# A state space layer on one core: ScalarE's work planned in a list of its own, products moved to other places, B's rows sent ahead of C's

## The chip, the cores and the metric

One core of a Trainium2 chip. The metric is the device time of the program in microseconds (us), the median of several executions. Ratios are computed as the mean time of one kernel's fast runs over the mean of the kernel before's fast runs of the same rounds, so they are not quite the ratio of the medians that stand beside them.

## The reference, cut to what matters

The program is two residual layers on an image of 4 x 384 x 64 x 64, float32: a state space layer, then attention over 7 x 7 windows. Only the first is touched.

```python
xn = layer_norm(group_norm(x))                  # 4 x 4096 positions x 384
xb, z = split(xn @ in_proj_w.T)                 # 768 channels each
xc = silu(conv4(xb) + conv_b)
dt, Bm, Cm = split(xc @ x_proj_w.T)             # 24, 16, 16
dt = softplus(dt @ dt_w.T + dt_b)
A = -exp(A_log)                                 # 768 x 16
def step(h, dt_t, B_t, C_t, x_t):               # over 4096 positions
    h = exp(dt_t[:, :, None] * A) * h + (dt_t * x_t)[:, :, None] * B_t[:, None, :]
    return h, sum_n(h * C_t)                    # 16 states n
y = (scan(step) + xc * D) * silu(z)
out = x + y @ out_proj_w.T
# ... then the attention layer, unchanged
```

## The kernel before

The layer runs in 64 *steps* (4 batches x 16 chunks of T = 256 positions). A step has 6 blocks of 128 channels (`d`) x 4 groups of 4 states (`g`), so 24 pairs (d, g), numbered `m`; each is scanned in two *halves* of two states. So a step has 48 halves, and one VectorE scan of 128 x 513 belongs to each.

For one half ScalarE makes two exponentials, VectorE scans; for one `m` there is one product dt x B (128 x 1024), 15 of the 24 on VectorE and 9 on GpSimd; GpSimd multiplies the states by C and TensorE sums them over the states into `y`. What VectorE reads lies in two PSUM tiles of two banks each. Half 0 of every `m` uses the first tile's exponentials, half 1 the second's; the copy of dt x for block `d` lies in tile `d % 2`:

```python
pairs  = [ps_a.tile([P, 4 * T], F32, name=f"pair_{k}") for k in range(2)]
dtx_ps = [t[:, 0:T] for t in pairs]             # dt x, copied there by ScalarE
da_ps  = [t[:, T : 3 * T + 1] for t in pairs]   # two exponentials

def driven(I, m, h, eng):                       # dt x B
    d, g = divmod(m, NS // NG)
    dtx = dtx_ps[d % 2] if eng is nc.vector else h["dtx"][d]
    eng.tensor_tensor(states(dbs[I, m]), dtx..., h["B"][g]..., ALU.mult)

def decay(I, m, half, h):                       # the two exponentials of a half
    for k in range(2):
        act(da_ps[half][:, k*(T+1) : k*(T+1) + T], h["dt"]..., AF.Exp, scale=...)

def scans(I, m, half, hs):
    nc.vector.tensor_tensor_scan(hs[:, half, :], da_ps[half], dbs[I, m][:, half, :], ...)
```

Everything else of a step (norms, projections, convolution, softplus, gating, output) is cut into small pieces, and a plan says after which half each piece is emitted. An engine executes its instructions in the order in which they are emitted here, so the plan *is* the schedule:

```python
plan = [[[] for _ in range(SLOTS)] for _ in range(STEPS + 3)]     # SLOTS = 48
driven_at = ((-4, 0), (-1, 1), (1, 1), (2, 1), ...)   # (half, on VectorE?) of each dt x B
turn(I, p, h, slot_of(I), (p + 1) * (SLOTS // 3) + 4, (3, 2, 4)[p])   # y leaves PSUM, p of 3
# ...
for half in range(2):
    decay(*nxt, steps[nxt[0]])       # exponentials of the next half
    if half == 0:
        with_c(*behind[-1])          # GpSimd: states x C
        for _ in range(ready):
            summed(*behind.pop(0))   # TensorE: sums of y
    scans(I, m, half, hs)            # VectorE
    run(I, 2 * m + half, 2 * m + half + 1)   # what is planned in this half
```

## Time and profile before

| kernel before | |
|---|---|
| time, median of 3 (lowest, highest) | 8,390.1 us (8,385.0, 8,392.5) |
| a usual step, from scan to scan 48 later | 92.4 us |
| of which VectorE idles (mean of steps 10 to 59) | 6.2 us |
| first and last scan of the layer | 117.9 and 6,044.3 us |

The step's length and the idle time by half come from counting scans off in the trace, 48 at a time, and adding VectorE's gaps before each instruction by the half in which it stands. A line of a timeline holds start, us, engine, line, operation, how many in a row. The busy line of the page (engine, us, share of the span, number of instructions) is needed again for the result:

```profile
PE 7235.9 (86%) x45882; PEld 5481.4 (65%) x45882; DVE 7052.0 (84%) x10231; ACT 5936.5 (71%) x15294; POOL 6966.1 (83%) x5719
```

ScalarE's largest waits between 1,000 and 5,000 us (who waited, for whom: us in total, times, longest):

```profile
ACT pair L96 <- DVE hs L594: 316.9, 536, 3.2
ACT pair L96 <- DVE db L575: 302.8, 172, 3.7
```

An exponential waits either for the scan that reads its tile, or for a product that reads the dt x part of the same tile. ScalarE is not the bound, so this costs nothing by itself. It says how tightly the two engines are laced together: whoever moves a product moves exponentials.

TensorE's timeline shortly before scan 20 of step 30, which starts at 2,940.66 (start, us, engine, line, operation, how many in a row).

```profile
2936.97 1.04 PE L623 MATMUL y<-ident,hs 128*128 128x128 f32 x8
2937.84 1.46 PE L389 MATMUL mm_ps<-xn,w_in 128*128 128x256 f32 x6
2939.14 1.46 PE L668 MATMUL mm_ps<-yg,w_out 128*128 128x256 f32 x6
2940.43 1.04 PE L623 MATMUL y<-ident,hs 128*128 128x128 f32 x8
```

The last eight matmuls finish a third of `y`. They are emitted in half 18, behind six matmuls of half 16 and six of half 17, and here they start 0.23 us *before* scan 20 (1.6 us before it in the median of steps 10 to 59). ScalarE copies this `y` out of PSUM in half 20, and right behind it on ScalarE stands the dt x copy that lies in the tile that scan 21 reads.

### The profile page before, as it was taken

To read this page: it belongs to the slowest core of one execution; us is meant where nothing else is said; L and a number is where in the kernel's file an instruction comes from. 1 tells how busy PE (TensorE), PEld (TensorE's weight loads), DVE (VectorE), ACT (ScalarE), POOL (GpSimd) and SP (SyncE) were. 2 spreads that over 40 slices of the span, in tenths; PEclk is the share of its full clock that TensorE was granted. 3 is DMA by queue.
4 is the path that set the end of the run, shared out by engine and by line. 5 is a ranking of instruction groups with operands and counts; after the bars stand their busy time and mean duration, and the time that the engine had idled before them with its cause. 6 is when DMAs were issued, how large, how long until landed. Compare 5 with 4: busy or idle time off the path is not lost.

```text
span 8390.6 us, 137885 instructions
## 1 busy us (share of the span) xinstructions
PE 7235.9 (86%) x45882; PEld 5481.4 (65%) x45882; DVE 7052.0 (84%) x10231; ACT 5936.5 (71%) x15294; POOL 6966.1 (83%) x5719
## 2 busy tenths in 40 slices
PE   6888888888888888888888888888699999999999
PEld 5766677667666766676667766767555555555555
DVE  5999999999999999999999999999756666666666
ACT  5788787878887788788878888888545455455455
POOL 4898898988998898898989898989767677777677
PEclk9998998888988898988899889998799999999999
DMA  3112211121112112211211111112132232232222
GB/s 108 63 59 65 75 59 54 62 73 59 62 65 73 52 57 64 74 57 64 68 62 52 56 64 62 53 58 69 63 92 87 76 96 86 78 91 85 83 87 65
DMA packets 327496, 582.99 MB, mean 69 GB/s; under 512 B 62940, under 2 KB 211180, under 8 KB 326660
## 3 DMA queue, kind: packets, MB, share of 16 engines
q1 hardware_dynamic: 326788, 574.17, 21.9%
q8 instruction: 369, 6.05, 0.3%
q14 instruction: 339, 2.78, 0.1%
HBM read 471.49 MB, written 84.73 MB: 66 GB/s over the span
## 4 chain that ended last, share of the span: by engine, by line
PE 29%; ACT 21%; DVE 19%; POOL 18%; issue 12%; DMA 0%; SPq 0%; POOLq 0%; DVEq 0%; ACTq 0%
POOL hs L607 11%; DVE hs L594 10%; ACT pair L96 10%; POOL db L575 5%; DVE db L575 4%; PE pt_ps L981 4%; PE lg_ps L950 3%; PE mm_ps L854 3%; PE mm_ps L1034 3%; PE mm_ps L887 3%; PE mm_ps L917 3%; PE pv_ps L1007 3%; PE pt_ps L995 2%; ACT spe L96 2%; ACT xc L96 1%
## 5 line engine op out<-in xcount | busy, mean ns | idle before, releaser
L594 DVE TENSOR_TENSOR_SCAN hs<-pair,state,db 128x513 f32<-128x513 f32 x2880 | 3570.7, 1272 | 279.5 <-ACT pair L96 136.5
L96 ACT ACTIVATE pair<-dt,nega 128x256 f32<-128x256 f32 x6144 | 2922.3, 477 | 1051.3 <-DVE hs L594 476.7
L607 POOL TENSOR_TENSOR hs<-hs,C 128x1024 f32<-128x1024 f32 x1536 | 3491.4, 2273 | 124.2 <-POOL state L604 0.6
L623 PE MATMUL y<-ident,hs 128*128 128x128 f32 x12288 | 1839.9, 302 | 755.5 <-POOL hs L607 725.5
L623 PEld LDWEIGHTS y<-ident,hs 128*128 128x128 f32 x12288 | 1580.4, 156 | 1107.3 <-POOL hs L607 948.0
L971 POOL TENSOR_SCALAR sg<-sg,rsum 128x308 f32<-128x308 f32 x1536 | 1623.0, 1075 | 637.4 <-DVE rsum L969 632.7
L575 POOL TENSOR_TENSOR db<-dtx,B 128x1024 f32<-128x1024 f32 x576 | 1368.1, 2375 | 0.4 <-ACT db L568 0.4
L389 PE MATMUL mm_ps<-xn,w_in 128*128 128x256 f32 x4608 | 1187.0, 404 | 93.3 <-ACT xb L96 62.3
L575 DVE TENSOR_TENSOR db<-pair,B 128x1024 f32<-128x1024 f32 x960 | 1153.2, 1207 | 68.5 <-ACT pair L96 68.5
L389 PEld LDWEIGHTS mm_ps<-xn,w_in 128*128 128x128 f32 x4608 | 908.1, 205 | 230.4 <-ACT xb L96 76.0
L96 ACT ACTIVATE sg<-sg,mx 128x308 f32<-128x308 f32 x1536 | 828.7, 540 | 251.4 <-DVE mx L956 224.1
L956 DVE CUSTOM_DVE_ANT_0 sg<-lg_ps,bias 128x308 f32<-128x308 f32 x1536 | 643.2, 475 | 382.5 <-PE lg_ps L950 382.5
L396 PE MATMUL mm_ps<-xb,dcv 128*128 128x256 f32 x3072 | 744.4, 389 | 111.2 <-DVE dt L527 107.0
L396 PEld LDWEIGHTS mm_ps<-xb,dcv 128*128 128x128 f32 x3072 | 578.3, 193 | 213.3 <-DVE dt L527 129.2
L604 POOL COPY state<-hs 128x4 f32<-128x4 f32 x1536 | 292.6, 190 | 477.8 <-DVE hs L594 464.6
L999 ACT COPY tb<-pt_ps 88x512 f32<-88x512 f32 x384 | 222.2, 579 | 624.7 <-PE pt_ps L995 624.7
L668 PE MATMUL mm_ps<-yg,w_out 128*128 128x256 f32 x2304 | 529.5, 380 | 0.0
L986 DVE COPY ta<-pt_ps 110x512 f32<-110x512 f32 x768 | 492.7, 683 | 23.3 <-PE pt_ps L981 23.3
L668 PEld LDWEIGHTS mm_ps<-yg,w_out 128*128 128x128 f32 x2304 | 428.6, 190 | 53.2
L981 PE MATMUL pt_ps<-ident,sg 128*110 128x128 f32 x3072 | 417.6, 279 | 0.9 <-POOL sg L971 0.8
L546 POOL TENSOR_TENSOR dtx<-dt,xc 128x256 f32<-128x256 f32 x384 | 281.6, 733 | 122.6 <-DVE dt L527 122.6
L981 PEld LDWEIGHTS pt_ps<-ident,sg 128*110 128x110 f32 x3072 | 322.7, 133 | 78.1 <-issue 49.0
(145 smaller groups left out, 9301.3 us busy)
## 6 DMA issues: line engine op xcount, KB each, us to landing
B<-bcrows SPq DMA_DIRECT2D x256, 512.0 KB
C<-bcrows SPq DMA_DIRECT2D x256, 512.0 KB
vw<-vd SPq DMA_DIRECT2D x1792, 33.0 KB
xr<-x SPq DMA_DIRECT2D x28, 1056.0 KB
vd<-v SPq DMA_DIRECT2D x280, 96.0 KB
xi<-in_x_dram SPq DMA_DIRECT2D x64, 384.0 KB
xo<-in_x_dram SPq DMA_DIRECT2D x64, 384.0 KB
x<-xo SPq DMA_DIRECT2D x64, 384.0 KB
```

The source lines that it names most:

```text
L96: ins = nc.scalar.activation(o, i, func, **kw)
L389: nc.tensor.matmul(pb[:, k, :], w_in[:, j, m * P : (m + 1) * P], xn[:, j, :], start=(j == 0), stop=(j == NJ - 1),)
L396: nc.tensor.matmul(pb[:, k, :], dcv[:, d, c, :], xb[:, d, c : c + T], start=(c == 0), stop=(c == KC - 1),)
L575: eng.tensor_tensor(states(db), dtx.unsqueeze(1).unsqueeze(1).broadcast_to([P, 2, 2, T]), h["B"][g].rearrange("p (a k) t -> p a k t", k=2) ...
L594: nc.vector.tensor_tensor_scan(hs[:, half, :], da_ps[half], dbs[I, m][:, half, :], state[d][g][:, 2 * half : 2 * half + 1] if I % NCHUNK e ...
L607: nc.gpsimd.tensor_tensor(by_state, by_state, h["C"][g].rearrange("p (a k) t -> p a k t", k=2), ALU.mult)
L623: nc.tensor.matmul(y[:, d % 2, half, :], hs[:, k // 2, at : at + P], ident, is_transpose=True, start=(first and half == 0 and d % 2 == 0), ...
L668: nc.tensor.matmul(h["po", first][:, m - first, :], w_out[:, d, m * P : (m + 1) * P], h["yg"][d // 2][:, d % 2, :], start=(d == 0), stop=( ...
L956: nc.vector.tensor_tensor_reduce(sg[:, hh, :], lg[:, :NK], bias[:, 4 * m + hh, :], -1.0, BIG, ALU.add, ALU.min, mx[:, hh : hh + 1],)
L971: nc.gpsimd.tensor_scalar(sg[:, hh, :], sg[:, hh, :], rs[:, hh : hh + 1], None, ALU.mult)
L981: nc.tensor.transpose(pt[: KN[c], col : col + P], sg[:, 2 * pair + hh, KOFF[c] : KOFF[c] + KN[c]], ident,)
L986: nc.vector.tensor_copy(t[: KN[0], :, :].rearrange("p a q -> p (a q)"), pt[: KN[0], :])
```

## The change

The intent, in its author's words: ScalarE's other work between exponentials and spread, dt x B laid where ScalarE has much to do, B transferred ahead of C. No instruction is added or removed. Each half of the plan gets two lists, one for ScalarE's work and one for the rest; multi-part ScalarE pieces are split so that single instructions can go between two exponentials; the places of dt x B are new.

```diff
+            ACT = 1
...
-                at(22, by_group)
+                for j in range(NJ):
+                    at(22 + j, lambda j=j: by_group(j), ACT)
...
-                at(35, root)
+                at(34, logged, ACT)
+                at(35, root, ACT)
...                             (biases, softplus parts: split in the same way)
-                    for tag in "BBBCBCCC":
+                    for tag in "BBBBCCCC":
...
-            plan = [[[] for _ in range(SLOTS)] for _ in range(STEPS + 3)]
+            plan = [[([], []) for _ in range(SLOTS)] for _ in range(STEPS + 3)]
...
-                def at(s, what):
-                    plan[I + s // SLOTS][s % SLOTS].append(what)
+                def at(s, what, kind=0):
+                    plan[I + s // SLOTS][s % SLOTS][kind].append(what)
...
             driven_at = (
-                (-4, 0), (-1, 1), (1, 1), (2, 1), (4, 0), (7, 1), (8, 0), (10, 1),
-                (12, 0), (15, 1), (17, 1), (18, 1), (20, 0), (22, 1), (24, 0), (26, 1),
-                (27, 1), (27, 1), (30, 0), (33, 1), (36, 0), (39, 1), (40, 0), (43, 1),
+                (-4, 0), (-2, 1), (-2, 1), (-1, 1), (3, 0), (5, 1), (7, 0), (7, 1),
+                (11, 0), (14, 1), (18, 1), (20, 1), (20, 0), (22, 1), (23, 0), (26, 1),
+                (27, 1), (28, 1), (30, 0), (32, 1), (36, 0), (38, 1), (39, 1), (40, 0),
             )
...
                 for half in range(2):
+                    acts, others = plan[I][2 * m + half]
                     if 2 * n + half + 1 < len(halves):
                         nxt = halves[2 * n + half + 1]
-                        decay(*nxt, steps[nxt[0]])
+                        acts.insert(0, lambda nxt=nxt: decay(*nxt, 0, steps[nxt[0]]))
+                        acts.insert(2, lambda nxt=nxt: decay(*nxt, 1, steps[nxt[0]]))
+                    for what in acts:
+                        what()
                     if half == 0:
...                             (states x C, sums of y: as before)
                     scans(I, m, half, hs)
-                    run(I, 2 * m + half, 2 * m + half + 1)
+                    for what in others:
+                        what()
```

One line does something other than it says. `at` files ordinary work under index 0 and ScalarE's under index 1; the loop unpacks index 0 as `acts`. So the list that is emitted between the exponentials, ahead of the scan, is the *ordinary* one.

More of the change, by code (lines that the diff above doesn't have):

```diff
@@ L346, in load, with by_group @@
                     )
-                def by_group():
-                    h["xn"] = w2.tile([P, NJ, T], F32, tag="xn", name=f"xn_{b}_{i}", bufs=1)
-                    for j in range(NJ):
-                        act(
-                            h["xn"][:, j, :], h["x"][:, j, :], AF.Identity,
-                            scale=gms[b][:, j, 1:2], bias=gbs[b][:, j, :],
-                        )
+                def by_group(j):
+                    if j == 0:
+                        h["xn"] = w2.tile([P, NJ, T], F32, tag="xn", name=f"xn_{b}_{i}", bufs=1)
+                    act(
+                        h["xn"][:, j, :], h["x"][:, j, :], AF.Identity,
+                        scale=gms[b][:, j, 1:2], bias=gbs[b][:, j, :],
+                    )
                 def mean(of, key):
@@ L371, in square, with logged @@
                     act(h["sq"], h["xn"], AF.Square)
+                def logged():
+                    act(h["var"][:, 0, :], h["var"][:, 0, :], AF.Ln, bias=eps)
                 def root():
-                    act(h["var"][:, 0, :], h["var"][:, 0, :], AF.Ln, bias=eps)
                     act(h["var"][:, 0, :], h["var"][:, 0, :], AF.Exp, scale=-0.5)
                 at(12, load)
-                at(22, by_group)
+                for j in range(NJ):
+                    at(22 + j, lambda j=j: by_group(j), ACT)
                 at(25, lambda: mean("xn", "mu"))
                 at(27, lambda: with_row("mu", ALU.subtract))
-                at(30, square)
+                at(30, square, ACT)
                 at(32, lambda: mean("sq", "var"))
-                at(35, root)
+                at(34, logged, ACT)
+                at(35, root, ACT)
                 at(36, lambda: with_row("var", ALU.mult))
@@ L399, in conv, with with_bias @@
                     )
-            def with_bias(dst, pb, bias):
-                for k in range(2):
-                    act(dst[:, k, :], pb[:, k, :], AF.Identity, bias=bias[:, k : k + 1])
+            def with_bias(k, dst, pb, bias):
+                act(dst[:, k, :], pb[:, k, :], AF.Identity, bias=bias[:, k : k + 1])
             def prepared(I, h, at):
@@ L436, in prepared, with x_out, conv_out, z_out @@
                     pair(("x", p), x, lambda pb, k, d=d: in_proj(pb, k, d + k, h["xn"]))
-                    at(x[2], lambda p=p, d=d: with_bias(
-                        xb[:, d : d + 2, KC - 1 :], h["pb"][("x", p)], binp[:, d : d + 2]
-                    ))
-                    def conv_out(p=p, d=d):
-                        c = w2.tile([P, 2, T], F32, tag="xc", name=f"xc_{b}_{i}_{d}", bufs=6)
-                        with_bias(c, h["pb"][("c", p)], cvb[:, d : d + 2])
-                        h["xc"].append(c)
-                    pair(("c", p), c, lambda pb, k, d=d: conv(pb, k, d + k))
-                    at(c[2], conv_out)
-                    def z_out(p=p, d=d):
-                        z = w2.tile([P, 2, T], F32, tag="sz", name=f"sz_{b}_{i}_{d}", bufs=6)
-                        with_bias(z, h["pb"][("z", p)], binp[:, ND + d : ND + d + 2])
-                        h["sz"].append(z)
+                    def x_out(k, p=p, d=d):
+                        with_bias(
+                            k, xb[:, d : d + 2, KC - 1 :], h["pb"][("x", p)], binp[:, d : d + 2]
+                        )
+                    def conv_out(k, p=p, d=d):
+                        if k == 0:
+                            h["xc"].append(
+                                w2.tile([P, 2, T], F32, tag="xc", name=f"xc_{b}_{i}_{d}", bufs=6)
+                            )
+                        with_bias(k, h["xc"][p], h["pb"][("c", p)], cvb[:, d : d + 2])
+                    pair(("c", p), c, lambda pb, k, d=d: conv(pb, k, d + k))
+                    def z_out(k, p=p, d=d):
+                        if k == 0:
+                            h["sz"].append(
+                                w2.tile([P, 2, T], F32, tag="sz", name=f"sz_{b}_{i}_{d}", bufs=6)
+                            )
+                        with_bias(k, h["sz"][p], h["pb"][("z", p)], binp[:, ND + d : ND + d + 2])
                     pair(("z", p), z, lambda pb, k, d=d: in_proj(pb, k, ND + d + k, h["xn"]))
-                    at(z[2], z_out)
+                    for k in range(2):
+                        at(x[2], lambda k=k, out=x_out: out(k), ACT)
+                        at(c[2], lambda k=k, out=conv_out: out(k), ACT)
+                        at(z[2], lambda k=k, out=z_out: out(k), ACT)
                 def burst():
@@ L488, in prepared @@
                 at(30, lambda: x_proj((3, 4, 5)))
-                at(33, rows)
+                at(33, rows, ACT)
                 def softplus(q, first):
@@ L502, in project, with part, onemore @@
                             )
-                    def parts():
-                        t["e"] = w2.tile([P, 2, T], F32, tag="sp_e", name=f"spe_{b}_{i}_{q}")
-                        t["r"] = w2.tile([P, 2, T], F32, tag="sp_r", name=f"spr_{b}_{i}_{q}")
-                        for k in range(2):
-                            bias = dtb[:, 2 * q + k : 2 * q + k + 1]
-                            act(t["e"][:, k, :], t["pb"][:, k, :], AF.Abs, bias=bias)
-                            act(t["r"][:, k, :], t["pb"][:, k, :], AF.Relu, bias=bias)
+                    def part(key, func, k):
+                        if k == 0:
+                            t[key] = w2.tile([P, 2, T], F32, tag=f"sp_{key}", name=f"sp{key}_{b}_{i}_{q}")
+                        act(
+                            t[key][:, k, :], t["pb"][:, k, :], func,
+                            bias=dtb[:, 2 * q + k : 2 * q + k + 1],
+                        )
                     def exped():
                         act(t["e"], t["e"], AF.Exp, scale=-1.0)
+                    def onemore():
                         act(t["pb"], t["e"], AF.Identity, bias=1.0)
@@ L530, in softplus @@
                     at(first, project)
-                    at(first + 3, parts)
-                    at(first + 4, exped)
-                    at(first + 5, logged)
+                    for k in range(2):
+                        at(first + 3, lambda k=k: part("e", AF.Abs, k), ACT)
+                        at(first + 3, lambda k=k: part("r", AF.Relu, k), ACT)
+                    at(first + 4, exped, ACT)
+                    at(first + 4, onemore, ACT)
+                    at(first + 5, logged, ACT)
                     at(first + 6, lost)
@@ L578, in driven, with decay @@
                 )
-            def decay(I, m, half, h):
+            def decay(I, m, half, k, h):
                 d, g = divmod(m, NS // NG)
-                for k in range(2):
-                    n = g * NG + 2 * half + k
-                    act(
-                        da_ps[half][:, k * (T + 1) : k * (T + 1) + T],
-                        h["dt"][d // 2][:, d % 2, :], AF.Exp, scale=nega[:, d, n : n + 1],
-                    )
+                n = g * NG + 2 * half + k
+                act(
+                    da_ps[half][:, k * (T + 1) : k * (T + 1) + T],
+                    h["dt"][d // 2][:, d % 2, :], AF.Exp, scale=nega[:, d, n : n + 1],
+                )
             def scans(I, m, half, hs):
@@ L654, in gated @@
                     h["yg"].append(yg)
-                at(s, out)
+                at(s, out, ACT)
                 at(s + back_at, back)
@@ L736, in layer0 @@
                     slot_of(I)(slot, lambda I=I, d=d, h=h: dt_x(I, d, h))
-                    slot_of(I)(slot + 2, lambda d=d, h=h: dt_x_copied(d, h))
+                    slot_of(I)(slot + 2, lambda d=d, h=h: dt_x_copied(d, h), ACT)
                 for m, (slot, vector) in enumerate(driven_at):
                     eng = nc.vector if vector else nc.gpsimd
-                    slot_of(I)(slot - 2, lambda I=I, m=m: opened(I, m))
+                    slot_of(I)(slot - 2, lambda I=I, m=m: opened(I, m), ACT)
                     slot_of(I)(slot, lambda I=I, m=m, h=h, eng=eng: driven(I, m, h, eng))
@@ L756, in layer0, with run @@
                     slot_of((b + 1) * NCHUNK)(SLOTS + 31 + 3 * n, part)
-            def run(I, a=0, z=SLOTS):
-                for slot in plan[I][a:z]:
-                    for what in slot:
+            def run(slot):
+                for kind in (ACT, 0):
+                    for what in slot[kind]:
                         what()
-            run(-2)
-            run(-1)
+            for slot in plan[-2] + plan[-1]:
+                run(slot)
             M = ND * NS // NG
             halves = [(I, m, half) for I in range(STEPS) for m in range(M) for half in range(2)]
-            decay(*halves[0], steps[0])
+            for k in range(2):
+                decay(*halves[0], k, steps[0])
             behind = []
@@ L790, in layer0 @@
                 summed(*what)
-            run(STEPS)
+            for slot in plan[STEPS]:
+                run(slot)
     def layer1(x1s, mvs, gms):
```

## The prediction

> **What bounds the kernel now.** I read the 40 slices first. They show two stages: slices 1 to 28 are the state space layer, about 5,900 of the 8,390 us, and the rest is the attention layer, which the change does not touch.
>
> ```profile
> DVE  5999999999999999999999999999756666666666
> ACT  5788787878887788788878888888545455455455
> ```
>
> Then the busy time by stretch inside the first stage.
>
> ```profile
> 1000.00:2000.00 1000.00, 840.09 (x4406) 701.43 (x4407) 932.35 (x915) 801.95 (x1967) 890.15 (x686) 0.89 0.19 64
> sum 4000.00, PE 3355.08 PEld 2789.24 DVE 3733.45 ACT 3215.13 POOL 3576.53; mean PE 838.77 PEld 697.31 DVE 933.36 ACT 803.78 POOL 894.13
> ```
>
> From 1,000 to 5,000 us VectorE is busy 93%, GpSimd 89%, TensorE 84%, ScalarE 80%. VectorE is the bound; it idles 267 us of 4,000. Counting scans in the timeline, 48 to a step (I call one scan with what is planned around it a half, numbered 0 to 47), a usual step lasts 92.4 us, of which VectorE idles 6.2. There are 64 steps, so even a perfect arrangement gains at most 6.2 x 64 = 397 us, 4.7% of the kernel. What VectorE waits for in those 4,000 us:
>
> ```profile
> DVE hs L594 <- ACT pair L96: 98.3, 188, 1.0
> DVE hs L594 <- ACT pair L552: 90.7, 126, 1.2
> DVE db L575 <- ACT pair L96: 47.1, 43, 1.4
> DVE yg L653 <- PE mm_ps L646: 13.9, 3, 4.6
> ```
>
> Nearly all is ScalarE: exponentials that come late behind its other work, and (L552) the copy of dt x into the same PSUM tile. No wait on a transfer is there. The timeline round ScalarE's longest burst (two table loads, six Silu) shows how the present order covers it:
>
> ```profile
> 3044.35 0.67 DVE L653 TENSOR_TENSOR yg<-mm_ps,sz 128x512 f32<-128x512 f32 x1
> 3044.93 1.22 DVE L575 TENSOR_TENSOR db<-pair,B 128x1024 f32<-128x1024 f32 x1
> 3046.06 1.28 DVE L594 TENSOR_TENSOR_SCAN hs<-pair,state,db 128x513 f32<-128x513 f32 x1
> 3047.26 0.40 DVE L682 TENSOR_TENSOR xo<-mm_ps,xo 128x256 f32<-128x256 f32 x1
> 3047.57 2.35 DVE L575 TENSOR_TENSOR db<-pair,B 128x1024 f32<-128x1024 f32 x2
> 3049.83 0.95 DVE L365 TENSOR_TENSOR xn<-xn,mm_ps 128x768 f32<-128x768 f32 x1
> 3050.70 1.28 DVE L594 TENSOR_TENSOR_SCAN hs<-pair,state,db 128x513 f32<-128x513 f32 x1
> 3052.34 2.46 DVE L594 TENSOR_TENSOR_SCAN hs<-pair,state,db 128x513 f32<-128x513 f32 x2 [0.36 <-ACT pair L96]
> ```
>
> While ScalarE is away, three dt x B products and other work keep VectorE going; only 0.36 us is lost.
>
> **What the Trainium skill says.** "PSUM — Partial Sum Buffer", section "PSUM bank collisions raise a hardware error": ScalarE and VectorE may not touch one bank and quadrant together, so accesses must be guarded by bank, not by address. Here dt x and the exponentials lie in one two-bank tile; the built program orders every access to that tile, and the trace agrees: exponentials waited 302.8 us, 172 times, for dt x B products that only read another part of the tile. The same page, "Engine vs sequencer instructions", calls the ScalarE and VectorE queues strict FIFO: one waiting instruction holds all behind it. "ScalarE: Activation LUTs", "What ACT_TABLE_LOAD costs": about 1,283 ns for a load (trace: 1,283), and activations back to back overlap by about 93 ns. The trace agrees: four 0.47 us softplus parts start 0.36 us apart, but the two exponentials of a half, of which the second waits for the first, start 0.47 apart. That is what the first part of the change is after.
>
> **The change part by part.** No instruction is added or taken away; ScalarE, VectorE and GpSimd do the same work. So all lies in order.
>
> (1) Exponentials apart. The plan now holds two lists per half: index 0 for ordinary work, index 1 for ScalarE's. The loop unpacks them as "acts, others", but index 0 is the ordinary list. So the names are swapped: the *ordinary* work of a half (VectorE, GpSimd, TensorE) goes between the exponentials and ahead of the scan, and ScalarE's work comes after, as before. The built order confirms it: the two exponentials still stand side by side on ScalarE, the gain of 0.11 us a pair does not come, and on VectorE every dt x B, softplus correction and gating product stands one scan earlier than its number says.
>
> (2) The places of dt x B were chosen for the intended order. With the swap, a product in half s on pair tile k waits, by the built program's semaphores, for the exponentials of half s if s and k agree in parity. Otherwise it stands after those of s+1 and waits for them, and they cannot start before scan s-1 ends: a sure bubble. Durations from the trace: scans follow every 1.19 us; exponentials start 1.32 us after the start of the scan that frees their tile (3007.32 to 3008.64); they take 0.98, and VectorE starts 0.04 later. So a product standing right after scan s-1 idles 1.32 + 0.98 + 0.04 - 1.19 = 1.15 us. This hits the products of halves 22, 26, 27, 38, and 47 (there between the two exponentials: one less, 0.65).
>
> (3) I walked one step by hand through the built order with these durations (dt x B 1.12, gating 0.58, corrections 1.33, xn 0.87; ScalarE: two bias adds 0.72, ys 0.48, dt x copy 0.30, parts 1.44, Exp and Identity 1.18, Ln 0.48, burst 5.84). Idle time of VectorE in us by half:
> - 46: 0.28 (product waits for the dt x copy of half 45); 47: 0.65;
> - 1: 0.90 and 43: 0.58 (the softplus correction, now ahead of its scan, waits for its Ln);
> - 5: 1.30 (product waits for ys and dt x copies);
> - 10: 0.42; 14: 0.35; 17: 0.42; 21: 0.10;
> - 22: 1.15; 26: 1.29; 27: 0.84; 38: 1.15;
> - 29: 1.37, the burst: exponentials of 28 end, then 5.84 + 0.98 us pass on ScalarE, while only products 16 and 17, xn and two scans, 5.5 us, are left for VectorE; before, gating and product 15 lay inside this window too;
> - 36: 0.58 (xn waits for the root).
>
> The sum is 11.4, against the measured 6.2 with (by half) 1.09 at 0, 0.79 at 5, 0.42 at 10, 0.52 and 0.48 at 14 and 15, 1.12 at 21, 0.71 at 41 as its large terms. The same walk through halves 7 to 24 of the kernel before gave 0.38, 0.8, 0.5 and 1.19 where 0.42, 0.52, 0.48 and 1.12 were measured, so it is good to some 0.3 us a bubble. VectorE's work in the walk is 85.0 us (without the two bn_stats of 0.6, which fall where it waits anyway); 85.0 + 11.4 = 96.4, against 92.4: 4.0 us a step, 4.0 x 64 = 256 us.
>
> (4) B ahead of C: VectorE and GpSimd wait for no B or C now; worth 0. (5) Splitting normalisation over halves 22 to 24 and the root over 34 and 35 takes 0.5 to 1.0 us of ScalarE out of half 22; in the walk the exponentials there wait for scans instead: 0.
>
> **Rivals.** (a) The intent comes true enough: products nearer ScalarE's busy stretches (38 to 47, 18 to 23) give exponentials time. For it: those are where the kernel before loses 0.71 and 1.12. Against it: products that wait for exponentials themselves hide nothing. If half of the idle time went: 8,390 - 200 = 8,190. (b) GpSimd becomes or relieves the bound: its products also move up, one hs x C (2.5 us) earlier; it is 89% busy and VectorE never waited for it, so this is 0 either way; were it to delay the scans, some 50 us more. (c) The bubbles cancel: a wait at 22 gives ScalarE the lead that it lacks at 24, and new waits only replace old ones. Idle time stays at 6 to 8 us: 8,390 to 8,500. For it: before has twelve small waits that shift freely. Against it: the walk carries ScalarE's lead along and still ends at 11.4.
>
> **Range and chances.** I shade 8,390 + 256 = 8,646 a little for (c): 8,630 us. A bubble error of 1.5 us a step is 96 us, and (c) has the longer tail below: 8,490 to 8,710. The 2% line is 8,558, a rise of 2.6 us a step, so slower has 0.73, within 2% 0.21, faster 0.06.
>
> **What would show it.** VectorE busy time unchanged at 7,050, its share of the first stage down from 93% to about 90%; the wait of dt x B products for exponentials up from 1.1 us a step to about 5, a new wait of them for the dt x copy of 1.5, a new wait of the softplus correction for Ln of about 1.5; the scan after the burst waiting about 1.4 instead of 0.36; exponentials waiting for products down from 7 us a step to about 1; exponentials still 0.47 us apart; GpSimd and transfers without new waits. A step of 92 us or less with the same order would prove the walk wrong, and exponentials apart by 0.36 or with other work between them would prove the reading of the swap wrong.

## The result, and the profile after

| | before | after |
|---|---|---|
| time, median of 4 runs | 8,389.8 us | 8,803.6 us (8,800.0 to 8,813.2) |
| ratio | | 1.0496 (95% interval 1.0477 to 1.0514): slower |
| a usual step | 92.4 us | 99.0 us |
| VectorE idle per step (mean of 10 to 59) | 6.2 us | 12.3 us |
| first and last scan | 117.9 and 6,044.3 us | 121.0 and 6,464.9 us |

The change costs 414 us, 174 more than predicted and 94 above the upper end of the range. The last scan is 421 us later, so all of it lies in the state space layer. Batch ends have no part in it: the few longer steps around each of the three add about 9 us before and 10 after.

The busy line of the page after, and VectorE's 40 slices:

```profile
PE 7386.3 (84%) x45882; PEld 5586.0 (63%) x45882; DVE 7090.7 (80%) x10231; ACT 5951.1 (68%) x15294; POOL 6970.7 (79%) x5719
...
DVE  5888888888888888888888888888856666666666
```

The same work, thinner: VectorE's nines have become eights in every slice of the layer. Its busy time rose by 39 us, 0.6 a step. That is not more work either. Two VectorE instructions that follow without a wait overlap by some 0.09 us (in step 30 a product starts at 3,136.44 and takes 1.20, and the scan after it starts at 3,137.55), and each new bubble takes one such overlap away: added up over the layer, the overlaps are 18 us less than before. The rest are instructions that came out a little longer, such as the products (a mean of 1,215 ns instead of 1,207). Busy time by stretch, 1,000 to 5,000 us (sum, then the mean of a stretch):

```profile
sum 4000.00, PE 3212.18 PEld 2654.94 DVE 3511.86 ACT 3008.09 POOL 3338.59; mean PE 803.05 PEld 663.74 DVE 877.96 ACT 752.02 POOL 834.65
```

VectorE is down from 93% to 88%. What it waits for in those 4,000 us, in which 40.4 steps lie:

```profile
DVE db L592 <- ACT pair L96: 183.4, 219, 1.3
DVE hs L610 <- ACT pair L569: 98.6, 40, 3.3
DVE hs L610 <- ACT pair L96: 74.9, 120, 1.4
DVE mm_ps L535 <- ACT dt L96: 47.5, 76, 0.8
DVE db L592 <- ACT pair L569: 47.1, 81, 1.2
```

The first, fourth and fifth lines are the predicted bubbles: products (`db`) waiting for exponentials, 4.5 us a step (183.4 / 40.4), the softplus correction waiting for its Ln, 1.2, and products waiting for the dt x copy, 1.2. The third holds the predicted waits of scans at halves 10, 17 and 29. The second was not predicted: 40 times, so once a step, a *scan* waits 2.5 us for the dt x copy. By half it is one place, scan 21. In the kernel before the same kind of wait came 126 times, none longer than 1.2 us; at scan 21 it was 1.12. VectorE there, in step 30 (a wait and its releaser in brackets):

```profile
3137.55 1.28 DVE L610 TENSOR_TENSOR_SCAN hs<-pair,state,db 128x513 f32<-128x513 f32 x1
...
3141.33 1.28 DVE L610 TENSOR_TENSOR_SCAN hs<-pair,state,db 128x513 f32<-128x513 f32 x1 [2.50 <-ACT pair L569]
3143.67 1.22 DVE L592 TENSOR_TENSOR db<-pair,B 128x1024 f32<-128x1024 f32 x1 [1.06 <-ACT pair L96]
```

ScalarE in the same moments:

```profile
3137.02 0.98 ACT L96 ACTIVATE pair<-dt,nega 128x256 f32<-128x256 f32 x2
...
3140.43 0.59 ACT L650 COPY ys<-y 128x512 f32<-128x512 f32 x1 [2.42 <-PE y L639]
3140.91 0.38 ACT L569 COPY pair<-dtx 128x256 f32<-128x256 f32 x1
```

The copy that scan 21 waits for stands behind the copy of `y`, and that one stood 2.42 us waiting for TensorE: the strict queue order that the prediction names, and the trace agrees with it. The exponentials that scan 21 reads had been done since 3,138.00, but they lie in the tile that the copy writes too, and the scan stands behind the copy. TensorE:

```profile
3133.30 2.75 PE L394 MATMUL mm_ps<-xn,w_in 128*128 128x256 f32 x12
3135.89 1.04 PE L639 MATMUL y<-ident,hs 128*128 128x128 f32 x8
3136.76 2.75 PE L684 MATMUL mm_ps<-yg,w_out 128*128 128x256 f32 x12
3139.36 1.04 PE L639 MATMUL y<-ident,hs 128*128 128x128 f32 x8
```

Read this against the four lines of the kernel before, also of step 30. There the sums of `y` began 0.23 us before scan 20, here they begin 1.8 us after it. In both, twelve matmuls stand between these sums and the ones before, but not the same twelve. Here they are the output-projection matmuls of halves 17 and 18. The six of half 18 stood *behind* the sums before; the swapped names put them ahead, as they put the products ahead of the scan. Six such matmuls take 1.30 us from start to start (2,937.84 to 2,939.14 in the kernel before). That is not all of the delay: in the mean of steps 10 to 59 the sums begin 1.8 us after scan 20 instead of 1.0 before it. Counted from scan 0 they come 1.2 us later, and VectorE gets to scan 20 1.6 us sooner (35.3 us instead of 36.9). Experiments 3 and 5 show what goes into this beside the order.

ScalarE's own waits confirm that it is one event a step:

```profile
ACT pair L96 <- DVE hs L610: 726.5, 806, 4.4
ACT ys L650 <- PE y L639: 92.9, 40, 2.6
```

### The profile page after: what moved, and what is told of

Same layout as the page of the kernel before. It is cut to its first block, busy times and chain, and to the rows that moved or that the text cites.

```text
span 8811.5 us, 138367 instructions
## 1 busy us (share of the span) xinstructions
PE 7386.3 (84%) x45882; PEld 5586.0 (63%) x45882; DVE 7090.7 (80%) x10231; ACT 5951.1 (68%) x15294; POOL 6970.7 (79%) x5719
## 5 line engine op out<-in xcount | busy, mean ns | idle before, releaser
L639 PE MATMUL y<-ident,hs 128*128 128x128 f32 x12288 | 1811.4, 299 | 766.6 <-POOL hs L623 759.7
L592 DVE TENSOR_TENSOR db<-pair,B 128x1024 f32<-128x1024 f32 x960 | 1160.8, 1215 | 377.5 <-ACT pair L96 294.9
L394 PEld LDWEIGHTS mm_ps<-xn,w_in 128*128 128x128 f32 x4608 | 940.8, 212 | 151.2 <-DVE gm_a L270 5.9
L401 PEld LDWEIGHTS mm_ps<-xb,dcv 128*128 128x128 f32 x3072 | 608.9, 202 | 95.2 <-DVE dt L541 0.8
L478 PE MATMUL mm_ps<-xc,w_xp 128*56 128x256 f32 x768 | 296.3, 565 | 169.8 <-ACT xc L96 169.8
```

The lines of the kernel that those rows point to most:

```text
L394: nc.tensor.matmul(pb[:, k, :], w_in[:, j, m * P : (m + 1) * P], xn[:, j, :], start=(j == 0), stop=(j == NJ - 1),)
L401: nc.tensor.matmul(pb[:, k, :], dcv[:, d, c, :], xb[:, d, c : c + T], start=(c == 0), stop=(c == KC - 1),)
L592: eng.tensor_tensor(states(db), dtx.unsqueeze(1).unsqueeze(1).broadcast_to([P, 2, 2, T]), h["B"][g].rearrange("p (a k) t -> p a k t", k=2) ...
L639: nc.tensor.matmul(y[:, d % 2, half, :], hs[:, k // 2, at : at + P], ident, is_transpose=True, start=(first and half == 0 and d % 2 == 0), ...
```

## The experiments

The theory after reading the traces: all of the loss is emission order. The swap makes products wait for exponentials, and, on TensorE, makes the sums of `y` late. Rivals: the new places are bad in themselves; the late copy at scan 21 has another cause than TensorE's order; the shared PSUM tile is innocent, and the products would wait anyway. Ten kernels ran; each was timed in three rounds, and each gave the right result. Each quoted expectation says for itself what it calls its theories. The medians of the kernel before beside them were 8,390.5, 8,390.1 and 8,392.6 us.

### 1. The sums of y first

Only TensorE's order is put back: the sums are emitted ahead of the ordinary list, the rest of the swap stays.

```diff
+                    newest = behind[-1:]
+                    if half == 0:
+                        ...
+                        for _ in range(ready):
+                            summed(*behind.pop(0))
                     for what in acts:
                         what()
                     if half == 0:
-                        if behind:
-                            with_c(*behind[-1])
-                        ...             (the sums)
+                        if newest:
+                            with_c(*newest[-1])
```

> The changed kernel, with TensorE's sums of y of a half emitted ahead of that half's ordinary work again, as they stood before the change; nothing else. Theory A (the term that the prediction left out: the copy of y on ScalarE in half 20 waits for TensorE, 2.3 us a step, because other matmuls now stand ahead of the sums): the wait of scan 21 falls from 2.50 us a step to about 0.1-0.3, a step from 99.0 to about 96.5, the kernel from 8,804 to about 8,650. Theory B (the copy waits because GpSimd is late with hs x C): the wait and the 8,804 stay within 30 us.

Measured: 8,689.3 us, ratio 1.0356 (1.0341 to 1.0372), 114 us less than the changed kernel. VectorE's wait at scan 21 fell from 2.50 to 0.41 us, idle time to 10.3 a step. What is left of the wait chain, first VectorE's line and then, in its own view, ScalarE's:

```profile
DVE hs L610 <- ACT pair L569: 17.9, 41, 1.3
```

```profile
ACT ys L650 <- PE y L639: 11.1, 41, 0.5
```

That is 39 us above the expected 8,650, but far more than the 30 us that theory B allowed. Every other wait kept its size. So without the swapped order on TensorE the unpredicted wait hardly comes about, and that is worth 114 us. The order does not make it alone, though (experiments 3 and 5). The other 300 us are still there.

### 2. The names put right

```diff
-                    acts, others = plan[I][2 * m + half]
+                    others, acts = plan[I][2 * m + half]
```

> The changed kernel with the two lists unpacked in the other order, so that ScalarE's work goes between the exponentials and ahead of the scan, and ordinary work comes after the scan, as the words of the change say. Theory A (the swap of the two lists makes the loss): most of the 414 us comes back, 8,300 to 8,500, products no longer wait over 1 us at halves 22, 26, 38, and the exponentials of a half have other work between them. Theory B (the places of dt x B are the loss, whichever way the lists go): it stays over 8,650.

Measured: 8,348.2 us, ratio 0.9948 (0.9933 to 0.9963). One pair of names is worth 455 us. It is also the only kernel so far in which ScalarE's order is what the change wanted:

```profile
3062.66 0.48 ACT L96 ACTIVATE pair<-dt,nega 128x256 f32<-128x256 f32 x1 [1.07 <-DVE db L592]
3063.07 0.61 ACT L96 ACTIVATE spe<-spe 128x512 f32<-128x512 f32 x1
3063.59 0.46 ACT L96 ACTIVATE pair<-dt,nega 128x256 f32<-128x256 f32 x1
3063.99 0.58 ACT L96 ACTIVATE mm_ps<-spe 128x512 f32<-128x512 f32 x1
```

The first exponential of a half is followed after 0.41 us by another instruction, and that one after 0.52 by the second exponential, where two neighbouring exponentials of one half start 0.49 to 0.51 apart. So the mechanism of the change is real. Yet the whole is worth only 0.5%, and VectorE still idles 5.0 us a step, with two waits of a new kind, 1.31 at scan 12 and 0.96 at scan 24:

```profile
3086.70 2.34 DVE L610 TENSOR_TENSOR_SCAN hs<-pair,db 128x513 f32<-128x513 f32 x2 [1.70 <-ACT pair L569]
```

The dt x copy is now ahead of the scan that reads the same tile, and the scan must wait for it. At scan 12 the copy in turn waits for GpSimd, which has only just made this dt x: 41.9 us in all between 1,000 and 5,000 us, 1.36 before the scan shown.

### 3. The swap with the old places

The changed kernel, with the places of dt x B of the kernel before.

```diff
             driven_at = (
-                (-4, 0), (-2, 1), (-2, 1), (-1, 1), (3, 0), ...
+                (-4, 0), (-1, 1), (1, 1), (2, 1), (4, 0), ...    (all 24 as before)
             )
```

> The changed kernel with the places of dt x B of the kernel before: the swapped lists alone. Theory A (a product that stands ahead of scan s and shares its tile with the exponentials of s+1 must idle about 1.1 us): ten of the fifteen old places are of that kind (47, 1, 10, 15, 17, 22, 26, 27 twice, 33) against five of the new ones, so idle time rises above the 12.3 us a step of the changed kernel, to 14 or more, and the time to 8,900 or more. Theory B (the new places are the loss): it falls to 8,400-8,600.

Measured: 8,982.4 us, ratio 1.0705 (1.0687 to 1.0723); idle 14.6 us a step. The products' wait for exponentials is the largest of all kernels, 315.4 us in 290 waits between 1,000 and 5,000 us. Its bubbles are 1.34 at half 10, 0.84 at 15, 1.06 at 17 and 22, 1.35 at 26, 0.46 at 27, 0.55 at 33 and 1.63 at 47: all eight where half and tile differ in parity, as the prediction's rule has it. A ninth place of that kind, half 1, shows none. So the swap hurts at either set of places, and the new ones hurt less. That the places are bad falls. One wait is missing: TensorE's order is swapped here too, but the copy of `y` waits for it only 0.6 us in all (92.9 in the changed kernel). VectorE needs 40.3 us here from scan 0 to scan 20, not 35.3, so that the sums, which begin 3.5 us before scan 20, are in time. In experiment 4 below, the new places without the swap, that copy waits 0.45 us a step. So the long wait needs the swap and the new places together.

### 4. The new places alone

The kernel before, with nothing but the new `driven_at`.

```diff
             driven_at = (
-                (-4, 0), (-1, 1), (1, 1), (2, 1), (4, 0), ...
+                (-4, 0), (-2, 1), (-2, 1), (-1, 1), (3, 0), ...  (all 24 as after)
             )
```

> The kernel before with the new places of dt x B alone, with its loop as it was. Theory A (the swap is the loss, the places are about neutral where a product follows its scan): 8,330 to 8,480, and no product waits 1 us at halves 22, 26 and 38. Theory B (the places are the loss): 8,600 or more.

Measured: 8,181.4 us, ratio 0.9751 (0.9737 to 0.9766), better than I expected. Idle time is 3.0 us a step, half of that of the kernel before, and a usual step is 88.9 us. VectorE's whole list of waits between 1,000 and 5,000 us:

```profile
DVE hs L594 <- ACT pair L552: 58.3, 104, 1.2
DVE hs L594 <- ACT pair L96: 54.5, 157, 1.0
DVE yg L653 <- PE mm_ps L646: 13.8, 3, 4.6
```

The wait of products for exponentials (47.1 us before) is gone, and the scans' waits have nearly halved. So the change holds one good part, 209 us, which the rest of it buries.

### 5. One product one half later

The product at half 38 falls under the parity rule: with the swap it stands after the exponentials of half 39 and must idle some 1.15 us. One half later it should not.

```diff
-                (27, 1), (28, 1), (30, 0), (32, 1), (36, 0), (38, 1), (39, 1), (40, 0),
+                (27, 1), (28, 1), (30, 0), (32, 1), (36, 0), (39, 1), (39, 1), (40, 0),
```

> The changed kernel with one product (number 21 of a step) moved from half 38 to half 39, where its tile is no longer the one of the exponentials that are written next; nothing else. Theory A (a product ahead of its scan idles because it waits for the exponentials of the next half in the same tile): the wait of 1.06 us at half 38 goes, some of it may come back at 41 to 43 where ScalarE is busy, 8,740 to 8,775 instead of 8,804. Theory B (ScalarE is simply behind there, wherever the product stands): the wait moves to half 39 and the time stays at 8,795 to 8,810.

Measured: 8,658.3 us, ratio 1.0320 (1.0305 to 1.0336), 145 us less than the changed kernel, for one number. The bubble of 1.06 at half 38 is gone and has not come up elsewhere, as the rule says: 1.06 x 64 = 68 us. The other part I did not foresee: the wait at scan 21 fell from 2.50 to 1.19, because ScalarE's copy of `y` waited for TensorE only 41.3 us in all instead of 92.9.

The traces show how. In both kernels TensorE waits near the beginning of a usual step for GpSimd. It then works through 180 recorded matmuls without a gap, the same ones in both, until it comes to the last sums of this `y`. The first eight after the wait, in step 30, are these in the changed kernel,

```profile
3104.99 1.97 PE L639 MATMUL y<-ident,hs 128*128 128x128 f32 x8 [4.34 <-POOL hs L623]
```

and these here:

```profile
3032.42 1.09 PE L639 MATMUL y<-ident,hs 128*128 128x128 f32 x8 [2.88 <-POOL hs L623]
```

The granted clock of TensorE was 0.50 between 3,105 and 3,109 us there, and 1.00 between 3,032.5 and 3,036.5 us here. The slow stretch costs 2 us, and since no gap follows, they are still there when TensorE comes to the sums. In the changed kernel the first 20 records after the wait take 6.3 us in the median step, here 4.0. Of the 50 steps 10 to 59 here, 29 have them done in under 4.2 us, and there scan 21 waits 0.60 us in the mean; in the other 21 it waits 2.0. So the 2.50 us at scan 21 come from the swapped order *and* a stretch at half the clock. With the order put back (experiment 1), scan 21 waits 0.5 us even in the 22 steps whose first 20 records take over 5 us. Why the half clock falls into this stretch less often here stays open.

### 6. Products from SBUF

If the products wait for exponentials only since dt x shares their PSUM tile, products that read dt x from SBUF will not wait. (The copies are still made, so that only one thing changes.)

```diff
-                dtx = dtx_ps[d % 2] if eng is nc.vector else h["dtx"][d]
+                dtx = h["dtx"][d]
```

> The changed kernel with VectorE's products reading dt x from the SBUF tile that GpSimd wrote, not from the copy in the exponentials' PSUM tile; the copies are still made. Theory A (the shared tile makes the waits): no product waits for an exponential or for the copy any more; 6 us a step of idle time go at halves 5, 14, 22, 26, 27, 38, 46, 47. If a product then takes 1.2 us as now, the time is near 8,450; if two SBUF inputs make products or GpSimd slower, part is given back and mean durations show it. Theory B (the products wait because ScalarE is late with everything): products' waits move to the scans behind them and idle time stays near 12 us.

Measured: 9,076.8 us, ratio 1.0819 (1.0801 to 1.0837): the slowest of all, and the theory holds nevertheless. No product waits for ScalarE any more, and VectorE's idle time falls from 12.3 to 4.2 us a step. But the product itself is another one. Its group between 1,000 and 5,000 us (count, then busy us, mean ns of one, then idle time before it), in the changed kernel:

```profile
L592 DVE TENSOR_TENSOR db<-pair,B 128x1024 f32<-128x1024 f32 x603 | 729.2, 1215 | 233.8 <-ACT pair L96 183.4 <-ACT pair L569 47.1
```

and in this one:

```profile
L592 DVE TENSOR_TENSOR db<-dtx,B 128x1024 f32<-128x1024 f32 x578 | 1175.6, 2039 | 0.0
```

From 1,215 to 2,039 ns, with a shortest of 1,191 and a longest of 3,420. 15 products by 0.82 us are 12.4 us a step; less the 8.1 of idle time saved that is 4.3, and the step grew by 4.0 (to 103.0). The Trainium skill's "SBUF — State Buffer", section "🔬 SBUF: two separate sides", tells why: VectorE and GpSimd share a pair of ports that is "an exclusive lock, not a bandwidth split", which a VectorE operation with two SBUF inputs takes against a GpSimd operation that reads SBUF, and the other one fully blocks. The trace agrees: 566 of 577 products start while a GpSimd instruction runs, and last until that one ends plus 1.07 to 1.11 us. The profile counts the blocked time as busy, not as idle. With dt x in PSUM, products take 1,196 to 1,228 ns whatever GpSimd does.

### 7. The intended order, with dt x copied after the scan

Experiment 2, with the dt x copy back among the work after the scan.

```diff
-                    slot_of(I)(slot + 2, lambda d=d, h=h: dt_x_copied(d, h), ACT)
+                    slot_of(I)(slot + 2, lambda d=d, h=h: dt_x_copied(d, h))
```

> The lists in the intended order, but the copy of dt x on ScalarE planned as ordinary work, behind its scan. Theory A (of that kernel's 5.0 us of idle time a step, 1.31 at half 12 and 0.96 at half 24 come from copies that write the tile of the very scan they now stand ahead of): both go, 8,348 falls by 100 to 145 us to 8,200-8,250. Theory B (those scans wait because ScalarE is late): the waits stay and the time is within 30 us of 8,348.

Measured: 8,269.9 us, ratio 0.9856 (0.9841 to 0.9871), 78 us less than experiment 2, where I had hoped for 100 or more. The waits at scans 12 and 24 are gone; 0.71 at 14 and 0.65 at 18 came instead. So the copy was put in the wrong list, and still the intended order stays 88 us behind the old loop with the new places.

### 8. B ahead of C alone

```diff
-                    for tag in "BBBCBCCC":
+                    for tag in "BBBBCCCC":
```

> The kernel before with the last part of B transferred ahead of the first of C, alone. No wait of VectorE or GpSimd for a transfer is in any profile so far: 8,380 to 8,400, the same within noise. If the order of transfers mattered, it would be over 15 us from 8,390.

Measured: 8,389.4 us, ratio 0.9998 (0.9984 to 1.0013). Nothing, as predicted.

### 9. A version that beats both: old loop, new places, y copied one half later

The largest wait left in experiment 4 is 0.78 us at scan 21, again the copy of `y` and behind it that of dt x. The copy of `y` moves by one half; what follows from it stays where it was.

```diff
-                    turn(I, p, h, slot_of(I), (p + 1) * (SLOTS // 3) + 4, (3, 2, 4)[p])
+                    turn(I, p, h, slot_of(I), (p + 1) * (SLOTS // 3) + 5, (2, 1, 3)[p])
```

> The kernel before with the new places of dt x B (8,181 alone) and the copy of y on ScalarE one half later (21, 37, 5 instead of 20, 36, 4), so that the copy of dt x no longer stands behind it. Theory A (scans 21, 5 and 37 wait 0.78, 0.35 and 0.25 us for the dt x copy only because the y copy stands in front): these go and part returns at 22 to 24; 8,100 to 8,150. Theory B (ScalarE is behind there by the same amount whatever the order): 8,175 to 8,190.

Measured: 8,163.9 us, ratio 0.9729 (0.9714 to 0.9743): the lowest time, but between what the two theories said, and its interval overlaps that of experiment 4, so that the 17 us between them are not sure. Scan 21 now waits 0.14, but 0.65 came up at 26; idle 2.7 us a step.

```profile
DVE hs L594 <- ACT pair L96: 84.0, 194, 1.0
...
DVE hs L594 <- ACT pair L552: 11.1, 38, 0.5
```

Against experiment 4 the wait for the copy fell by 47 us and that for exponentials rose by 30. Waits for ScalarE move rather than vanish once they are this small.

### 10. The same in the intended order

Experiment 7 with the edit of experiment 9, to see whether the intended order catches up.

> The intended lists with the dt x copy behind its scan (8,270 alone) and the y copy one half later. If the interleaved exponentials were worth keeping, this ends below the kernel above. Theory A (they are not: the saved 0.1 us a pair lies on an engine that is idle 18% and the second exponential comes later behind a foreign instruction): 8,200 to 8,265, above the other. Theory B: 8,100 or less.

Measured: 8,267.6 us, ratio 0.9850 (0.9834 to 0.9867): no gain on experiment 7, just above the range expected, 104 us behind experiment 9. Scan 14 waits 1.00 and 18 waits 0.67. ScalarE's work between exponentials, which must come *before* the scan, delays the second exponential, and so the scan; the 0.1 us that it saves on ScalarE saves an engine that is not the bound. That last sentence is my reading of the waits; no run takes the cost apart further.

### All runs

| kernel | us | VectorE idle per step |
|---|---|---|
| before | 8,389.8 | 6.2 |
| after | 8,803.6 | 12.3 |
| 1 after, sums of y first | 8,689.3 | 10.3 |
| 2 after, names put right | 8,348.2 | 5.0 |
| 3 after, old places | 8,982.4 | 14.6 |
| 4 before, new places | 8,181.4 | 3.0 |
| 5 after, one product later | 8,658.3 | 9.9 |
| 6 after, products from SBUF | 9,076.8 | 4.2 |
| 7 as 2, dt x copied after the scan | 8,269.9 | 3.9 |
| 8 before, B first | 8,389.4 | 6.2 |
| 9 as 4, y copied later | 8,163.9 | 2.7 |
| 10 as 7, y copied later | 8,267.6 | 4.0 |

The parts nearly add up: new places alone -209, swap alone (experiment 3 against before) +592, together +383, and the change measured +414. That is partly chance. At scan 21 the parts would give 1.09 + 0.78 - 1.12 = 0.75 us a step where 2.50 were measured, 112 us too little, and other waits make up for most of it.

## Why the prediction was right in kind and wrong in size

**The swap, part (1): right.** In the trace of the changed kernel the two exponentials of a half are still neighbours on ScalarE, and products, corrections and gating stand one scan earlier. Experiment 2 shows that the names alone are worth 455 us. A small misreading: two exponentials of a half start 0.49 to 0.51 us apart in both kernels; 0.47 is how long one takes.

**The sure bubble, part (2): right.** It said 1.15 us at halves 22, 26, 27 and 38, and 0.65 at 47; measured are 1.06, 1.25, 0.46, 1.06 and 0.57. Experiment 5 took one away by the rule, experiment 6 took all away by parting the tiles, and experiment 3 moved them.

**The walk, part (3): here it failed, in the term of half 21.** The prediction put 0.10 us there; the trace has 2.50. The walk carried VectorE and ScalarE along, and took "ys 0.48" as a copy that starts when ScalarE comes to it. It had itself written that the swap moves "VectorE, GpSimd, TensorE", and then never asked what stood in front of what on TensorE. Six matmuls more than before stood in front of the sums of `y`, and TensorE came to them late besides, after a stretch at half the clock (experiment 5). Experiment 1 shows the size: without that wait the kernel takes 8,689 us, which is inside the predicted range; with it, 8,804, which is not.

The other terms were good to 0.4 us a bubble: 5 (0.90 measured, 1.30 predicted), 1 (0.76, 0.90), 43 (0.41, 0.58), 29 (1.23, 1.37), 36 (0.29, 0.58), 10, 14, 17 and 46 within 0.12. Nearly all were a little too large. Together without half 21 they came out at 9.8 of measured idle time against 11.3 predicted.

**The sum, also part (3): a base that did not match.** The prediction added its idle time to 85.0 us of VectorE work from the walk and compared the result with a *measured* 92.4. But the kernel before measures 92.9 us a step in the mean of steps 10 to 59, of which 6.2 are idle: its work is 86.7, not 85.0. A walk has to be compared with the same walk of the kernel before, or only its idle time with idle time: (11.4 - 6.2) x 64 = 333 us, not 256. And the changed kernel's work is 87.3 by the same account (99.6 - 12.3), the longer busy time told above. For the mean step, 99.6 measured against 96.4 predicted: +2.4 half 21, -1.5 all other bubbles, +1.7 the base, +0.6 busy time, in sum +3.2. So without half 21 the prediction would have been near for reasons that partly cancel.

**Parts (4) and (5).** B ahead of C is worth nothing: right, experiment 8. The splitting of ScalarE's pieces was never run alone and stays open.

**The rivals.** (a), that the products' new places give exponentials time, was given little, "half of the idle time" at most and 8,190 us. Under the swap that did not come about. Alone it came about almost to the letter: experiment 4, 3.0 of 6.2 us, 8,181 us. (b), GpSimd: it has two new waits, of 1.1 us a step for ScalarE's small copy of the kept state and of 0.9 for TensorE's sums, where "without new waits" stood; no scan of the changed kernel waits for GpSimd, so it is harmless. (c), bubbles that cancel: they did not under the swap. But experiments 7, 9 and 10 show it among small waits, where one removed brings another up.

**What would show it.** VectorE's share 88%, not "about 90%"; products for exponentials 4.5 us a step ("about 5"), for the copy 1.2 ("1.5"), correction 1.2 ("about 1.5"), scan after the burst 1.23 ("about 1.4"); exponentials for products from 7.0 to 1.2 ("about 1"). VectorE's busy time 7,091, not 7,050. Of all the things that the list names to look at, none is on TensorE.

What stays open: why TensorE's half-clock stretches fall where they do; and what in the intended order costs the 88 us by which experiment 7 stays behind experiment 4.

## What to carry to other kernels

Where emission order is the schedule, walk *every* in-order queue that feeds the bound, also the ones with room to spare: an engine at 80% delays another as soon as something stands in front of the one result that is waited for, and a queue that runs without gaps keeps a delay that it got long before. Compare a walk with a walk of the kernel before, never with its measurement, and try the parts of a change alone: here a faster kernel (-2.5%) lay inside a slower one (+5%). And a copy that looks like waste, dt x into PSUM, may be what keeps two engines from blocking each other.

## What the Trainium skill lacked or had wrong

- "PSUM — Partial Sum Buffer", "PSUM bank collisions raise a hardware error": says that accesses must be guarded by bank, not what the guard costs in a stream. Here eight of the 15 products of a step, which share a tile with exponentials and stand ahead of a scan, idle 0.35 to 1.25 us each in the mean, 5.7 us a step in all ((183.4 + 47.1) / 40.4).
- "Perfetto Trace Analysis", "Optimization Strategy": names too few buffers as what a gap that repeats can mean. Here 12.3 us of gaps repeat in every step with buffers unchanged, and emission order alone makes them 14.6, 12.3, 5.0 or 3.0 (experiments 3, the changed kernel, 2 and 4).
- No page tells that an in-order TensorE with idle time left can hold up a chain of two other engines by its order: with six matmuls (1.30 us) put ahead of eight, a scan waited 2.50 us a step; with the order put back, 0.41, and the kernel was 114 us faster (experiment 1).
- "SBUF — State Buffer", "🔬 SBUF: two separate sides": agrees with the trace, but has no figure for a stream in which both engines work all the time; here the product's mean rose from 1,215 to 2,039 ns, and a product lasted until the GpSimd instruction that it met ended, plus 1.07 to 1.11 us (experiment 6).
- "Perfetto Trace Analysis", "Optimizing Scalar/DVE Operations": tells that the last part of an instruction overlaps the next one, and the trace agrees (0.09 us between a product and a scan). It lacks that a wait loses this overlap on top of its own length: some 18 of the 39 us by which VectorE's busy time rose here, with the same instructions.
